# A fused scan, attention and feed-forward kernel: the two heads' TensorE products issued one behind the other

## The chip, the core and the metric

The kernel runs on one core of one Trainium2 chip. The metric is the device time of one execution in microseconds (us). TensorE is PE in the profile, its weight loads PEld, VectorE is DVE, ScalarE is ACT, GpSimd is POOL, and SyncE (SP) issues most of the DMAs. `s`, `pt`, `av`, `y`, `f` and so on are tiles; a number behind L is a line of the kernel.

## The reference, cut to what matters

The input is x of shape (8, 384, 32, 32) in float32: eight images of 1024 tokens with 384 channels. Layer 0 is a bidirectional state-space scan with 16 states per channel, a depthwise convolution and a gate. Layer 1 is causal attention with six heads of 64 channels, then a feed-forward part with quantized activations (the feed-forward part is zero for the last three images). The attention, which the change touches:

```python
scores = jnp.einsum('bhqd,bhkd->bhqk', q, k)
causal = jnp.tril(jnp.ones((T, T), dtype=bool))
scores = jnp.where(causal, scores, -jnp.inf)
attn = jax.nn.softmax(scores, axis=-1)
out = jnp.einsum('bhqk,bhkd->bhqd', attn, v)
```

## The kernel before

Channels lie on the partitions, 128 at a time, so an image has three blocks `c` of channels and a block holds two heads, `e` = 0 on partitions 0 to 63 and `e` = 1 on 64 to 127. The tokens are cut in halves `g` or `h` of 512 and in tiles of 128.

The scan is cut into 768 units of two states each. For a unit POOL multiplies (L587, `g`), ACT makes two exponentials (L600, `da`), DVE scans twice (L605), POOL multiplies again (L611), and PE transposes `g` into the PSUM bank `y` with eight products (L619). The tile `g` has six buffers; a buffer is free again when PE has transposed it. When the last state of a channel block is summed, `s_gate` (L640) builds `yb` in a PSUM bank with PE and DVE reads it (L667).

Attention of one image goes through the three blocks `c` and the two halves `g`. `scores` (L768) handles 128 queries and up to 512 keys for both heads: a score product per head (L779, contracting 64 partitions), on the diagonal a mask added by a further product (L788), then per head the negated row maximum on DVE (L798) and the exponential with its row sum on ACT (L799). The score tiles `ss` of the two heads take both banks of the tag `s`. `weighted_values` (L809) turns the probabilities with PE transposes into the two banks of the tag `pt` (L851), copies them on ACT (L853, `ptn`), and `weigh` (L856) multiplies them with the values (L863): both heads write one bank `av`, each its own half of the partitions. `spread` (L830) lays the row factors out in a bank `f` (L836), which ACT copies (L843).

PSUM has eight banks: one for `y`, two for `da`, two for `s`, two for `pt`, one for `av` (L95). The helper `bank` (L98) takes a tag; without a tag it takes `s` and `pt` in turn, so that `f` and `yb` fall on either. The feed-forward part takes `s`, and the preparation of later images' scans takes `pt` and `av`.

What sets the order: the program is written as lists of steps with assumed times (in us), and the lists are merged by those times (`spread_over` L1069, `timed` L1145), so that scan units, attention, feed-forward and the preparation of later images are woven together. The framework's scheduler then fixes each engine's order when the program is built, by the order in which instructions were written, by what is ready in its own model, and by two handles: `tc.high_priority(offset=n)` treats instructions as if they had been written n instructions earlier, and `pin` (`tc.keep_in_program_order`) lets an instruction follow the one written just before it on the same engine; other instructions may still come between. An engine then takes its instructions strictly in the fixed order. The last image's attention (L1157) runs without a scan beside it.

Of the kernel before, what the change touches and what calls it, by code (L numbers as in the profile page):

```python
# [2 lines left out]

# [37 lines left out]
PARTS = ((0, 0), (0, 1), (1, 1), (1, 0))  # L41
JOINT = 0.6
SET = 8
AHEAD = 2
ORDER = (0, 1, 2, 3, 5, 6, 4, 7)
LOG_EXP = "natural_log_exp_and_others"
# [7 lines left out]
def kernel(  # L54
# [43 lines left out]
    def bank(name, tag=None):  # L98
        if tag is None:
            turn[0] += 1  # L100
            tag = ("s", "pt")[turn[0] % 2]
        return ps.tile([P, HB], F32, name=name, tag=tag, bufs=BANKS[tag])
# [4 lines left out]
    def chunk(c):  # L107
        return slice(c * P, (c + 1) * P)
# [531 lines left out]
    def s_gate(u):  # L640

        if not u.last:
            return
        b, c, h = u.b, u.c, u.h
        yts = sst.pop(("yt", b, c, h))
        both = []
        for what in ("us", "z"):
            t = sp.tile([P, HB], F32, name=f"{what}h_{u.name}", tag=what, bufs=1)
            load(t, spilled[b, what, c][:, half(h)])
            both.append(t)  # L650
        us, sz = both
        tp = bank(f"yb_{u.name}")
        nc.tensor.matmul(
            out=tp, lhsT=diagd[:, c, :], rhs=us, start=True, stop=False, skip_group_check=True
        )
        for yt in yts:
            for i in range(QT):
                nc.tensor.matmul(
                    out=tp[:, chunk(i)],
                    lhsT=yt[:, i, :],  # L660
                    rhs=ident,
                    is_transpose=True,
                    start=False,
                    stop=(yt is yts[-1] and i == QT - 1),
                    skip_group_check=True,
                )
        nc.vector.tensor_tensor(sz, sz, tp, ALU.mult)  # L667
        t = dram.tile([P, HB], F32, name=f"sgy_{u.name}", tag=f"sp_gy_{c}_{h}")
        nc.sync.dma_start(out=t, in_=sz)
        spilled[b, "gy", c, h] = t  # L670


    def attention(b, emit_ffn, emit):
# [80 lines left out]

        def rows_of(e):
            return slice(e * HD, (e + 1) * HD)

# [3 lines left out]
        def probabilities(c, g, steps):  # L763


            nb = g + 1

            def scores(i, qi, n, kb, k0, k1):  # L768
                pr = mtile(f"pr_{b}_{c}_{qi}_{kb}").rearrange("p (e l) -> p e l", e=2)
                st["pr", c, g, i, kb] = pr  # L770
                if kb == 0 and i == 0:
                    for what in ("nm", "rs"):
                        st[what, c, g] = small.tile(
                            [P, QT, 2, nb], F32, name=f"{what}_{b}_{c}_{g}", tag=f"{what}{nb}"
                        )
                nm, rs = st["nm", c, g], st["rs", c, g]
                ss = [bank(f"s_{b}_{c}_{qi}_{kb}_{e}", "s") for e in range(2)]
                for e in range(2):
                    nc.tensor.matmul(  # L779
                        out=ss[e][:, : k1 - k0],  # L780
                        lhsT=st["q"][rows_of(e), c, chunk(qi)],
                        rhs=st["k"][rows_of(e), c, k0:k1],
                        start=True,
                        stop=(k1 < n),
                    )
                if k1 == n:
                    for e in range(2):
                        nc.tensor.matmul(  # L788
                            out=ss[e][:, k1 - k0 - P : k1 - k0],
                            lhsT=identb,  # L790
                            rhs=cmaskb,
                            start=False,
                            stop=True,
                        )
                for e in range(2):
                    s = ss[e][:, : k1 - k0]
                    m = nm[:, i, e, kb : kb + 1]
                    nc.vector.tensor_reduce(m, s, AX.X, ALU.max, negate=True)  # L798
                    nc.scalar.activation(  # L799
                        pr[:, e, : k1 - k0], s, AF.Exp, bias=m, accum_out=rs[:, i, e, kb : kb + 1]  # L800
                    )

            for i in range(QT):
                qi = g * QT + i
                n = (qi + 1) * P
                for kb, (k0, k1) in enumerate(blocks_of(n)):
                    steps(lambda i=i, qi=qi, n=n, kb=kb, k0=k0, k1=k1: scores(i, qi, n, kb, k0, k1))

        def weighted_values(c, g, steps):  # L809


            last = (g + 1) * QT - 1

            def factors():

                nm, rs = st["nm", c, g], st["rs", c, g]
                st["f", c, g] = mtile(f"f_{b}_{c}_{g}").rearrange("p (k l) -> p k l", k=2)
                if g == 0:
                    nc.vector.reciprocal(rs, rs)
                    return  # L820
                low = small.tile([P, QT, 2, 1], F32, name=f"low_{b}_{c}", tag="low")
                nc.vector.tensor_reduce(low, nm, AX.X, ALU.min)
                nc.vector.tensor_tensor(nm, low.to_broadcast([P, QT, 2, 2]), nm, ALU.subtract)
                nc.scalar.activation(nm, nm, AF.Exp)
                nc.vector.tensor_tensor(rs, rs, nm, ALU.mult)
                nc.vector.tensor_reduce(low, rs, AX.X, ALU.add)
                nc.vector.reciprocal(low, low)
                nc.vector.tensor_tensor(rs, nm, low.to_broadcast([P, QT, 2, 2]), ALU.mult)

            def spread(kb):  # L830

                fp = bank(f"f_{b}_{c}_{g}_{kb}")
                for i in range(QT):
                    for e in range(2):
                        f = st["rs", c, g][:, i, e, kb : kb + 1]
                        nc.tensor.matmul(  # L836
                            out=fp[rows_of(e), chunk(i)],
                            lhsT=f.to_broadcast([P, HD]),
                            rhs=ident,
                            start=True,  # L840
                            stop=True,
                        )
                nc.scalar.copy(st["f", c, g][:, kb, :], fp)  # L843

            def turned(j):
                cols = slice(max(j - g * QT, 0) * P, HB)
                for e in range(2):
                    pt = bank(f"pt_{b}_{c}_{g}_{j}_{e}", "pt")
                    for i in range(max(j - g * QT, 0), QT):
                        pr = st["pr", c, g, i, j // QT]  # L850
                        nc.tensor.transpose(pt[:, chunk(i)], pr[:, e, chunk(j % QT)], ident)  # L851
                    ptn = ptp.tile([P, HB], F32, name=f"ptn_{b}_{c}_{g}_{j}_{e}", tag=f"ptn{e}")
                    nc.scalar.copy(ptn[:, cols], pt[:, cols])  # L853
                    st["ptn", j, e] = ptn

            def weigh(j):  # L856
                if j % QT == 0:
                    st["av"] = bank(f"av_{b}_{c}_{g}_{j}", "av")
                av = st["av"]
                cols = slice(max(j - g * QT, 0) * P, HB)  # L860
                for e in range(2):
                    hd = 2 * c + e
                    nc.tensor.matmul(  # L863
                        out=av[rows_of(e), cols],
                        lhsT=st["v"][:, j, hd * HD : (hd + 1) * HD],
                        rhs=st["ptn", j, e][:, cols],
                        start=(j % QT == 0),
                        stop=(j % QT == QT - 1),
                    )
                if j % QT < QT - 1:  # L870
                    return
                kb = j // QT
                o, f = st["o"][:, c, half(g)], st["f", c, g][:, kb, :]
                if kb == 0:
                    nc.vector.tensor_tensor(o, av, f, ALU.mult)  # L875
                else:
                    nc.vector.tensor_tensor(av, av, f, ALU.mult)
                    nc.vector.tensor_tensor(o, o, av, ALU.add)

            for j in range(last + 1):  # L880

                @steps
                def _(j=j):
                    if j == 0:
                        factors()
                    if j % QT == 2:
                        spread(j // QT)
                    turned(j)
                    if j > 0:
                        weigh(j - 1)  # L890

            @steps
            def _():
                weigh(last)
# [314 lines left out]
```

## Time and profile before

| what | us |
|---|---|
| median of 4 runs (lowest, highest) | 5205.45 (5194.56, 5219.49) |
| the profiled execution, and its span | 5209.51, 5207.7 |
| busy PE, DVE, ACT, POOL in the span | 4286.2, 3568.9, 2717.6, 3688.5 |
| score products L779, mask products L788, `av` products L863 (busy) | 467.4, 75.7, 384.7 |
| transposes `y` L619 (busy) | 937.2 |
| attention's seven stretches together | 1987 |

The stretches are those between an image's first score product and its last `av` product: 925 to 1159, 1630 to 1877, 2330 to 2587, 3047 to 3302, 3755 to 4360 (two images), 4478 to 4699 and 5020 to 5188 us. A row of the timeline gives start, length, engine, line, operation, tile written and tiles read, shapes and the number of instructions that were merged; in brackets stands the idle time of the engine before it and what ended it. One float32 product of one head shows as two instructions. A row of the waits gives who waited, for whom, the total, how often and the longest. The granted clock is the share of full TensorE speed.

### The profile page before, as it was taken

The numbers are of one execution on the slowest core, as the hardware profiler recorded it, in microseconds if no ns is written. First come the engines' busy times: TensorE is split into PE (matmuls) and PEld (weight loads), VectorE is DVE, ScalarE is ACT, GpSimd is POOL, SyncE is SP. The second block draws the span as 40 slices with busy tenths as digits, with TensorE's granted clock in tenths as the row PEclk, the third lists the DMA queues.
The fourth block names the chain that finished last, engine by engine and source line by source line (L and its number), as shares of the span: only waits on it lengthen the run. The fifth ranks groups of instructions, "written<-read, shape, count | busy, mean of one in ns | idle before, by whom it ended". The sixth has DMA issues, their size and how long they took to land.

```text
span 5207.7 us, 51029 instructions
## 1 busy us (share of the span) xinstructions
PE 4286.2 (82%) x16842; PEld 2247.5 (43%) x16842; DVE 3568.9 (69%) x4205; ACT 2717.6 (52%) x4898; POOL 3688.5 (71%) x1944
## 2 busy tenths in 40 slices
PE   3677787888878888888887888978888888888799
PEld 1333344444434444444443444434444444444444
DVE  6887887667886577876677856678766655565522
ACT  4565564555644556545555445465454454463334
POOL 0578677886678776887776787677878977787600
PEclk7788787989888899888898898988999989999899
DMA  6554545324463234543243632335433234224200
GB/s 234 204 180 152 195 170 181 112 82 153 151 215 108 85 111 137 193 146 112 101 145 126 209 128 94 102 131 198 142 119 129 89 106 159 85 74 152 82 35 25
DMA packets 365009, 696.38 MB, mean 134 GB/s; under 512 B 30104, under 2 KB 88904, under 8 KB 364744
## 3 DMA queue, kind: packets, MB, share of 16 engines
q1 hardware_dynamic: 355232, 676.97, 38.4%
q10 hardware_dynamic: 9512, 16.15, 0.9%
q8 instruction: 133, 2.18, 0.2%
q14 instruction: 132, 1.08, 0.1%
HBM read 527.33 MB, written 165.68 MB: 133 GB/s over the span
## 4 chain that ended last, share of the span: by engine, by line
POOL 36%; PE 20%; DVE 17%; issue 17%; ACT 6%; DMA 3%; SPq 0%; POOLq 0%; ACTq 0%; DVEq 0%
POOL g L587 19%; POOL g L611 17%; DVE g L605 6%; PE qp L724 3%; PE y L619 3%; PE av L863 2%; PE s L779 2%; PE yp L1024 2%; DVE loc L399 2%; DVE dp L525 2%; PE pt L851 1%; PE ap L920 1%; DVE du L527 1%; DVE u L368 1%; PE op L694 1%
## 5 line engine op out<-in xcount | busy, mean ns | idle before, releaser
L587 POOL TENSOR_TENSOR g<-ud,bc 128x1024 f32<-128x1024 f32 x768 | 1835.0, 2389 | 753.7 <-PE y L619 604.3
L611 POOL TENSOR_TENSOR g<-g,bc 128x1024 f32<-128x1024 f32 x768 | 1819.2, 2369 | 255.0 <-DVE g L605 205.2
L600 ACT ACTIVATE da<-dl,amat 128x512 f32<-128x512 f32 x1536 | 1058.5, 692 | 1615.4 <-DVE g L605 1584.7
L605 DVE TENSOR_TENSOR_SCAN g<-da,carry,g 128x512 f32<-128x512 f32 x768 | 954.8, 1271 | 488.2 <-POOL g L587 453.8
L605 DVE TENSOR_TENSOR_SCAN g<-da,g 128x512 f32<-128x512 f32 x768 | 905.9, 1209 | 532.9 <-POOL g L587 510.6
L619 PE MATMUL y<-ident,g 128*128 128x128 f32 x6144 | 937.2, 300 | 274.5 <-POOL g L611 206.1
L619 PEld LDWEIGHTS y<-ident,g 128*128 128x128 f32 x6144 | 777.7, 155 | 704.2 <-issue 331.8
L779 PE MATMUL s<-k,q 64*128 64x512 f32 (+3 forms) x1152 | 467.4, 601 | 163.3 <-ACT pr L799 142.4
L798 DVE TENSOR_REDUCE nm<-s 128x1 f32<-128x512 f32 (+3 forms) x576 | 300.5, 545 | 247.7 <-PE s L788 182.3
L799 ACT ACTIVATE pr<-s,nm 128x512 f32<-128x512 f32 (+3 forms) x576 | 328.8, 574 | 146.5 <-DVE nm L798 145.6
L863 PE MATMUL av<-ptn,v 128*64 128x512 f32 (+3 forms) x1152 | 384.7, 565 | 24.2 <-DVE o L875 23.7
L979 PE MATMUL hp<-t,w 128*128 128x512 f32 x720 | 340.1, 616 | 32.4 <-ACT h L987 10.6
L851 PE MATMUL pt<-ident,pr 128*128 128x128 f32 x1728 | 309.7, 301 | 48.5 <-ACT ptn L853 25.3
L1024 PE MATMUL yp<-h,w 128*128 128x512 f32 x720 | 328.8, 614 | 11.2 <-DMA w<-w2s 6.3
L340 PE MATMUL in<-xn,win 128*128 128x512 f32 x576 | 293.9, 654 | 52.7 <-DVE xc L462 16.5
L853 ACT COPY ptn<-pt 128x512 f32<-128x512 f32 (+3 forms) x576 | 261.3, 479 | 122.1 <-PE pt L851 120.6
L779 PEld LDWEIGHTS s<-k,q 64*128 64x128 f32 x1152 | 163.4, 206 | 329.7 <-ACT pr L799 212.1
L724 PE MATMUL qp<-t,wqk 128*128 128x512 f32 x576 | 270.3, 620 | 23.7 <-DVE t L301 18.2
L851 PEld LDWEIGHTS pt<-ident,pr 128*128 128x128 f32 x1728 | 207.1, 151 | 180.3 <-ACT ptn L853 84.5
L399 DVE SCALAR_TENSOR_TENSOR loc<-xn,vec,loc 128x496 f32<-128x496 f32 (+3 forms) x384 | 259.4, 721 | 21.7 <-ACT loc L388 20.4
L610 POOL COPY carry<-g 128x2 f32<-128x2 f32 x384 | 83.5, 218 | 230.3 <-DVE g L605 230.3
L1024 PEld LDWEIGHTS yp<-h,w 128*128 128x128 f32 x720 | 140.2, 199 | 179.4 <-issue 167.4
(158 smaller groups left out, 4844.5 us busy)
## 6 DMA issues: line engine op xcount, KB each, us to landing
bc<-rows SPq DMA_DIRECT2D x512, 512.0 KB, 4.1
dl<-sdl SPq DMA_DIRECT2D x160, 256.0 KB, 2.9
ud<-sud SPq DMA_DIRECT2D x160, 256.0 KB, 2.7
t<-st SPq DMA_DIRECT2D x63, 512.0 KB, 5.3
su<-u SPq DMA_DIRECT2D x48, 512.0 KB, 2.9
du<-su SPq DMA_DIRECT2D x96, 256.0 KB, 4.2
sdl<-du SPq DMA_DIRECT2D x96, 256.0 KB, 3.3
sud<-du SPq DMA_DIRECT2D x96, 256.0 KB, 2.7
```

Of the source, the lines that this page charges most:

```text
L399: nc.vector.scalar_tensor_tensor(to, tap, vec[:, c, V_DW + k : V_DW + k + 1], to, ALU.mult, ALU.add)
L587: pin(nc.gpsimd.tensor_tensor(g, ud, sst["bc", 0, u.b, u.part, u.n], ALU.mult))
L600: nc.scalar.activation(da, sst["dl", u.b, u.c, u.part], AF.Exp, scale=amat[:, u.c, n : n + 1])
L605: nc.vector.tensor_tensor_scan(gi[:, ::step], da[:, ::step], gi[:, ::step], first, ALU.mult, ALU.add)
L611: pin(nc.gpsimd.tensor_tensor(g, g, sst["bc", 1, u.b, u.part, u.n], ALU.mult))
L619: nc.tensor.matmul(out=y[:, j, :], lhsT=g[:, i, chunk(j)], rhs=ident, is_transpose=True, start=(u.opens and i == 0 and j == 0), stop=(u.cl ...
L724: nc.tensor.matmul(out=qp, lhsT=st["wqk"][:, c, o : o + P], rhs=st["xn"][:, c, half(h)], start=(c == 0), stop=(c == NC - 1),)
L779: nc.tensor.matmul(out=ss[e][:, : k1 - k0], lhsT=st["q"][rows_of(e), c, chunk(qi)], rhs=st["k"][rows_of(e), c, k0:k1], start=True, stop=(k ...
L851: nc.tensor.transpose(pt[:, chunk(i)], pr[:, e, chunk(j % QT)], ident)
L863: nc.tensor.matmul(out=av[rows_of(e), cols], lhsT=st["v"][:, j, hd * HD : (hd + 1) * HD], rhs=st["ptn", j, e][:, cols], start=(j % QT == 0 ...
L979: nc.tensor.matmul(out=hp, lhsT=st["w1"][:, c, chunk(m % 2)], rhs=st["xn"][:, c, half(h)], start=(c == 0), stop=(c == NC - 1),)
L1024: nc.tensor.matmul(out=yp, lhsT=st["w2", k // 6][:, k % 6, :], rhs=st["h", k // NC][:, k % NC, half(h)], start=(k == 0), stop=(k == NF - 1),)
```

## The change

The second head's product is given a priority 400 instructions earlier and is pinned behind the first head's, and head 1 comes first, in the score products and in the `av` products. The masks are pinned behind both score products, head 1's first. Head 1's exponential is pinned behind head 0's. `yb` and `f` always take the tag `pt`, so the turn between `s` and `pt` shifts for the tiles that still alternate.

```diff
+HURRY = 400
...
-        tp = bank(f"yb_{u.name}")
+        tp = bank(f"yb_{u.name}", "pt")
...
+        def at_once(second):
+            return tc.high_priority(offset=HURRY) if second else nullcontext()
...
-                for e in range(2):
-                    nc.tensor.matmul(
-                        out=ss[e][:, : k1 - k0],
-                        lhsT=st["q"][rows_of(e), c, chunk(qi)],
-                        rhs=st["k"][rows_of(e), c, k0:k1],
-                        start=True,
-                        stop=(k1 < n),
-                    )
+
+                order = (1, 0)
+                for e in order:
+                    with at_once(e == order[1]):
+                        mm = nc.tensor.matmul(
+                            out=ss[e][:, : k1 - k0],
+                            lhsT=st["q"][rows_of(e), c, chunk(qi)],
+                            rhs=st["k"][rows_of(e), c, k0:k1],
+                            start=True,
+                            stop=(k1 < n),
+                        )
+                    if e == order[1]:
+                        pin(mm)
                 if k1 == n:
-                    for e in range(2):
-                        nc.tensor.matmul(
+                    for e in order:
+                        mm = nc.tensor.matmul(
...
                         )
+                        pin(mm)
                 for e in range(2):
...
-                    nc.scalar.activation(
+                    exp = nc.scalar.activation(
                         pr[:, e, : k1 - k0], s, AF.Exp, bias=m, accum_out=rs[:, i, e, kb : kb + 1]
                     )
+                    if e == 1:
+                        pin(exp)
...
-                fp = bank(f"f_{b}_{c}_{g}_{kb}")
+                fp = bank(f"f_{b}_{c}_{g}_{kb}", "pt")
...
-                for e in range(2):
+                for e in (1, 0):
                     hd = 2 * c + e
-                    nc.tensor.matmul(
...
+                    with at_once(e == 0):
+                        mm = nc.tensor.matmul(
...
+                    if e == 0:
+                        pin(mm)
```

More of the change, by code (lines that the diff above doesn't have):

```diff
@@ L1 @@
 import itertools
-from contextlib import ExitStack
+from contextlib import ExitStack, nullcontext
 import concourse.bass as bass
@@ L860, in weigh @@
                 cols = slice(max(j - g * QT, 0) * P, HB)
-                for e in range(2):
+                for e in (1, 0):
                     hd = 2 * c + e
[L863 to L869, printed above, removed]
+                    with at_once(e == 0):
+                        mm = nc.tensor.matmul(
+                            out=av[rows_of(e), cols],
+                            lhsT=st["v"][:, j, hd * HD : (hd + 1) * HD],
+                            rhs=st["ptn", j, e][:, cols],
+                            start=(j % QT == 0),
+                            stop=(j % QT == QT - 1),
+                        )
+                    if e == 0:
+                        pin(mm)
                 if j % QT < QT - 1:
```

## The prediction

> **What bounds the kernel now.** I read the page's chain of work first, then the waits of POOL and of PE, then busy time by stage, and last the timeline of PE, where the two heads' products can be seen.
>
> The chain that ended last, by line, on the page:
>
> ```profile
> POOL 36%; PE 20%; DVE 17%; issue 17%; ACT 6%; DMA 3%; SPq 0%; POOLq 0%; ACTq 0%; DVEq 0%
> POOL g L587 19%; POOL g L611 17%; DVE g L605 6%; PE qp L724 3%; PE y L619 3%; PE av L863 2%; PE s L779 2%; PE yp L1024 2%; DVE loc L399 2%; DVE dp L525 2%; PE pt L851 1%; PE ap L920 1%; DVE du L527 1%; DVE u L368 1%; PE op L694 1%
> ```
>
> The scan's two POOL products lead. But POOL is not always at work; the waits of POOL, longest first (total, times, longest):
>
> ```profile
> POOL g L587 <- PE y L619: 604.3, 226, 10.2
> ```
>
> So a POOL product waits 604 us for PE's transposes `y`, which free the buffers of `g`. PE issues in order, so whatever stands ahead of those transposes delays POOL. The waits of PE:
>
> ```profile
> PE y L619 <- POOL g L611: 206.1, 85, 14.3
> PE s L779 <- ACT pr L799: 142.4, 119, 6.0
> ```
>
> POOL and PE wait for each other; PE's second largest wait is for a score bank that the exponential has not yet released. I then took the seven stretches in which attention runs (columns: stretch, length, busy PE, PEld, DVE, ACT, POOL, granted clock, DMA share, GB/s); the first, the last and the sum:
>
> ```profile
> 925.00:1159.00 234.00, 194.09 (x1035) 106.91 (x1034) 152.01 (x191) 135.75 (x318) 193.17 (x100) 0.88 0.28 94
> ...
> 5020.00:5188.00 168.00, 158.63 (x707) 69.44 (x706) 48.65 (x104) 82.12 (x230) 0.00 (x0) 0.91 0.03 10
> sum 1987.00, PE 1690.03 PEld 911.88 DVE 1186.20 ACT 1074.95 POOL 1440.12; mean PE 241.43 PEld 130.27 DVE 169.46 ACT 153.56 POOL 205.73
> ```
>
> In the first six PE is busy 1531 of 1819 us (84%) and POOL 1440 (79%); in the last there is no scan, and PE has 94%. PE work taken out of these stretches shortens the last one nearly whole and the others in part; POOL leaves room for it, 379 us.
>
> Now what the change is about. PE's timeline, a tied product of each kind, and one that is not:
>
> ```profile
> 992.46 1.08 PE L863 MATMUL av<-ptn,v 128*64 128x512 f32 x4
> ...
> 1012.04 1.13 PE L779 MATMUL s<-k,q 64*128 64x512 f32 x4
> ```
>
> ```profile
> 1018.51 1.79 PE L779 MATMUL s<-k,q 64*128 64x512 f32 x4 [2.75 <-ACT pr L799]
> ...
> 1025.80 1.07 PE L863 MATMUL av<-ptn,v 128*64 128x512 f32 x2
> ```
>
> One head's product is two instructions, so x4 is a pair and x2 is one head. The pair at 992.46 takes 1.08 us, and so does the single head at 1025.80: two heads side by side on different halves of the array cost what one costs. The pair at 1018.51 has nothing between its heads, yet takes 1.79: its second head waited for its bank.
>
> Counted in the trace (a tied pair's two heads start within 45 ns): of 288 score pairs 88 run side by side, 68 follow each other with the second one late, 132 have other PE work between the heads. Of 288 `av` pairs 179 run side by side and 109 don't.
>
> **Part 1, the `av` products (L863).** The transposed probabilities of head 0 are copied by ACT ahead of head 1's. Today head 0's product may go when its copy is there, and older work slips in before head 1's. The change issues head 1 first, whose input comes last, and head 0 right behind it; then both inputs are there, and I expect all 109 to run side by side. By shape, untied pairs by what one head holds PE (start to start at high clock): 51 of 512 by 1.00, 22 of 384 by 0.80, 28 of 256 by 0.58, 8 of 128 by 0.37: 51.0 + 17.6 + 16.2 + 3.0 = **88 us of PE**. Cost: the first product now waits for the second copy (0.585 us for 512 columns, L853); behind it in PE's queue stand transposes and `y`, but a copy made for step j is used one step later, and PE and its weight loads wait for such a copy at `av` only 2.5 us in all, so I put the wait at 0 and its bound at 109 x 0.585 = 64 us.
>
> **Part 2, the score products (L779, L788).** Untied: 102 of 512 by 1.06, 30 of 384 by 0.84, 30 of 256 by 0.63, 38 of 128 by 0.42, which is 108.1 + 25.2 + 18.9 + 16.0 = 168 us if every one of the 200 ran side by side, 0.84 each. It can't be taken whole. Both need a bank of the tag `s`, which has two, and these come free one after the other, when ACT has done head 0's exponential and then head 1's. What keeps a pair apart is mostly that, and priority does not bring the second bank sooner. What the tie does bring is that the two maxima and the two exponentials then follow each other closely, so that the banks of the next pair come free closely too: today a late second head makes a late exponential and again a late second head. I take the 132 split pairs: half run side by side, 66 x 0.84 = 55; half become like the pair at 1018.51, which costs 1.79 in place of twice 1.06, about 0.38 of the gain, 66 x 0.32 = 21. The 68 that already follow each other stay. Sum **76 us**, bounds 0 and 168.
>
> The second product's priority lets it pass older PE work, `y` among it; that work then waits one product, at most 1.06 us, and no PE work is added: 0. The masks (L788) are tied behind both products. Head 0's maximum then waits for head 1's product as well, up to 1.06 us later than now where the pair was split; DVE is at 65% and has the scan to do meanwhile. I put it at 0.
>
> **Part 3, `f` and `yb` leave the banks of `s` for those of `pt`.** By PE's waits, `s` waits for `yb`'s reader 9.5 us (DVE zh L667) and, at 512 columns, for `f`'s 4.9 (ACT f L843); `pt` waits for `f`'s reader 16.4 and for `yb`'s 5.9. About half of the `f` and `yb` were in `pt` already, so the first sum goes and the second may double: -14.4 + 22.3, so I take **8 us** lost, bounds -25 and +25. Other tiles that take `s` and `pt` in turn change places; nothing in the trace prices that, and it lies within the same bounds.
>
> **Part 4, the exponential of head 1 tied behind head 0's.** They run in that order wherever I looked; 0.
>
> Sum of PE work: 88 + 76 - 8 = 156 us less. The last stretch holds about 15% of it (its untied heads hold PE 85 us of the 555 that all untied heads hold, both lines) and takes it whole: 24. In the others a part turns into waits for exponentials, which come no sooner: I take 0.65 of 132, that is 86, between 0.4 (53) and 1 (132). Together 110. The profiled execution took 5209.5 us around a span of 5207.7: 5209.5 - 110 = 5099.5. The median of the runs shown, 5205.45, is 4 us below the profiled one, hence about **5095 us**.
>
> A denser PE might be granted less clock: the same form took 1.78 us at 1022.60 and 1.07 at 1025.80. The stretches' means run from 0.84 to 0.92; a shift of 0.02 on 1690 us of PE work is 38 us either way, and is in the range.
>
> One rule speaks against the score term. An exponential of 512 columns takes 0.680 us and its accumulator's reading 0.196, so a pair holds ACT 1.75 us, more than the 1.06 of its product. The Trainium skill, TensorEngine Tiling, section PSUM Bottleneck, says that tiling speeds up TensorE but not the emptying of PSUM. By that rule the 76 us would be nothing and the result that of the first rival below; by the rows, ACT is busy 136 of 234 us in the first stretch and so bounds a single pair, not the stage.
>
> **The rivals.**
> *Only `av` is tied in effect.* For: 119 waits of `s` on `pr`, the two banks. Against: the 88 pairs that do run side by side now, with the same banks. 88 us of PE, by the same conversion (13 in the last stretch, 0.65 of 75): 62 off the median, 5143.
> *Nearly all is tied.* If close exponentials keep the banks together, 88 + 168 = 256 us of PE, 38 of them in the last stretch and 0.65 of 218: 180 off, 5025. Against: the 68 pairs that follow each other today and still wait.
> *Slower: the tie locks the banks.* A pair takes both banks and gives both back late, and PE, in order, stands before the pair with `y` behind it and POOL behind `y`. Price: one exponential with its reading, 0.876 us, for half of the 252 pairs beside the scan is 110, less the 62 of `av`: 48 more, about 5253. It decides once the idle time before L779 grows from 142 us by more than the 156 us of work removed. For it: the longest such wait is already 6.0 us.
> *The tie does nothing.* The scheduler may find no free bank and put other work between as before, with the bank moves costing what `av` gains: 5205.
>
> **The numbers.** Forecast 5095 (5050 to 5125), 0.40; only `av`, 0.24; nearly all, 0.15; slower, 0.13; nothing, 0.08. The range reaches from 4995 (most of the third case) to 5215 (the last and all of `av`). A measurement of this kernel tells about 0.3%, 16 us, from no change: faster 0.79, same 0.08, slower 0.13.
>
> **What would show it.** PE's busy time on L863 falls from 384.69 us by about 90, on L779 from 467.43 by about 75; rows of x2 become x4 with about 1.1 us; POOL's wait for `y` falls from 604 by about 80; the last stretch falls from 168 to about 145. If L779's busy time stays and PE's wait for `pr` stays, the first rival holds; if that wait passes 300 us, the slower one. I am wrong in the conversion if PE's busy time falls as said and the span does not.

## The result and the profile after

The changed kernel takes 5217.41 us (median of 49 runs, 5199.11 to 5234.35), the kernel before 5206.28 us (73 runs). The ratio is 1.0021, with a 95% interval of 1.0015 to 1.0027: a loss of 0.2%, which counts as no change by the bound of 0.3% that the prediction set, where it forecast 2.1% less. The profiled execution took 5210.11 us with a span of 5208.3.

The chain of work that ended last, on the page of the changed kernel:

```profile
POOL 39%; PE 18%; DVE 17%; issue 17%; ACT 5%; DMA 3%; SPq 0%; POOLq 0%; ACTq 0%; DVEq 0%
POOL g L588 19%; POOL g L612 19%; DVE g L606 5%; PE qp L725 3%; PE yp L1039 2%; PE y L620 2%; PE pt L863 2%; DVE loc L400 2%; PE s L786 2%; PE av L876 1%; DVE dp L526 1%; PE ap L935 1%; DVE u L369 1%; DVE du L528 1%; PE hp L994 1%
```

The `av` products fell from 2% to 1%, the transposes `pt` rose from 1% to 2%, and POOL's share grew from 36 to 39%. The groups of the two kinds of product (busy us and mean ns, then the idle time before them):

```profile
L786 PE MATMUL s<-k,q 64*128 64x512 f32 (+3 forms) x1152 | 426.5, 638 | 197.2 <-ACT pr L809 187.6 <-DVE v L750 4.9 <-ACT v L750 4.2
...
L876 PE MATMUL av<-ptn,v 128*64 128x512 f32 (+3 forms) x1152 | 273.7, 559 | 32.6 <-ACT ptn L865 31.9 <-DVE o L890 0.6
```

`av` is busy 111 us less than before (384.7), the score products 41 us less (467.4). So the change does what it says. But the waits did not shrink. POOL's for PE, then PE's (total, times, longest):

```profile
POOL g L588 <- PE y L620: 622.1, 176, 18.8
```

```profile
PE s L786 <- ACT pr L809: 187.6, 122, 6.5
PE pt L863 <- ACT ptn L865: 82.0, 60, 5.2
```

POOL waits 622 us for the transposes in place of 604, less often and longer at a time; PE waits 45 us longer for score banks and 57 us longer for the copies of the transposed probabilities. The stretches with attention, the first, the last and the sum of seven (length, busy PE, PEld, DVE, ACT, POOL, granted clock, DMA share, GB/s):

```profile
922.00:1164.00 242.00, 181.45 (x1040) 109.35 (x1039) 157.56 (x195) 138.25 (x322) 198.80 (x103) 0.87 0.26 89
...
5016.00:5192.00 176.00, 148.83 (x708) 70.20 (x708) 47.16 (x104) 80.10 (x229) 0.00 (x0) 0.79 0.03 10
sum 1979.00, PE 1571.64 PEld 915.05 DVE 1209.58 ACT 1066.39 POOL 1442.52; mean PE 224.52 PEld 130.72 DVE 172.80 ACT 152.34 POOL 206.07
```

PE is busy 118 us less in them, and they are 8 us shorter. The last one, with no scan to wait for, became longer (168 to 176 in these windows), with its clock down from 0.91 to 0.79.

**Where the gain went.** Busy time times mean granted clock is taken here as a rough measure of PE's work at full clock. The score tie is what the change does to the score products, masks and exponentials, the `av` tie what it does to the `av` products. The three profiled executions:

| | before | changed | without the score tie (e5) |
|---|---|---|---|
| span | 5207.7 | 5208.3 | 5136.4 |
| PE busy | 4286.2 | 4178.4 | 4206.2 |
| granted clock | 0.883 | 0.870 | 0.880 |
| work (busy x clock) | 3785 | 3635 | 3701 |
| span less busy | 921.5 | 1029.9 | 930.2 |

From before to the changed kernel work fell by 149.5, which at the old clock is 169 us of busy time. 61 us of it came back because the clock was lower (4178.4 less 3635.2/0.883), and 108 us became idle time: -169 + 61 + 108 = 0. In e5, described below, less work is taken out (94 us at the old clock), but only 14 us come back by the clock and 9 us as idle time, and 71 us remain. This is bookkeeping with mean clocks, not yet a cause; added up piece by piece over the clock records, work fell by 149 as well.

### The profile page after: what moved, and what is told of

Its sections match the earlier page's. It is cut to its first block, busy times and chain, and to the rows that moved or that the text cites. A ratio compares the mean times of both kernels' runs of the same rounds, so it can differ in the third digit from the quotient of the medians.

```text
span 5208.3 us, 51090 instructions
## 1 busy us (share of the span) xinstructions
PE 4178.4 (80%) x16842; PEld 2259.5 (43%) x16842; DVE 3595.5 (69%) x4206; ACT 2702.2 (52%) x4891; POOL 3687.3 (71%) x1944
## 3 DMA queue, kind: packets, MB, share of 16 engines
q14 instruction: 132, 1.08, 0.1%
## 4 chain that ended last, share of the span: by engine, by line
POOL 39%; PE 18%; DVE 17%; issue 17%; ACT 5%; DMA 3%; SPq 0%; POOLq 0%; ACTq 0%; DVEq 0%
POOL g L588 19%; POOL g L612 19%; DVE g L606 5%; PE qp L725 3%; PE yp L1039 2%; PE y L620 2%; PE pt L863 2%; DVE loc L400 2%; PE s L786 2%; PE av L876 1%; DVE dp L526 1%; PE ap L935 1%; DVE u L369 1%; DVE du L528 1%; PE hp L994 1%
## 5 line engine op out<-in xcount | busy, mean ns | idle before, releaser
L620 PE MATMUL y<-ident,g 128*128 128x128 f32 x6144 | 954.2, 303 | 299.9 <-POOL g L612 234.3
L620 PEld LDWEIGHTS y<-ident,g 128*128 128x128 f32 x6144 | 801.9, 157 | 645.5 <-POOL g L612 351.2
L786 PE MATMUL s<-k,q 64*128 64x512 f32 (+3 forms) x1152 | 426.5, 638 | 197.2 <-ACT pr L809 187.6
L863 PE MATMUL pt<-ident,pr 128*128 128x128 f32 x1728 | 336.2, 315 | 94.8 <-ACT ptn L865 82.0
L863 PEld LDWEIGHTS pt<-ident,pr 128*128 128x128 f32 x1728 | 217.9, 158 | 269.4 <-ACT ptn L865 169.5
L876 PE MATMUL av<-ptn,v 128*64 128x512 f32 (+3 forms) x1152 | 273.7, 559 | 32.6 <-ACT ptn L865 31.9
L1039 PEld LDWEIGHTS yp<-h,w 128*128 128x128 f32 x720 | 139.0, 197 | 176.0 <-issue 164.8
```

The costliest lines, as they stand in the source:

```text
L620: nc.tensor.matmul(out=y[:, j, :], lhsT=g[:, i, chunk(j)], rhs=ident, is_transpose=True, start=(u.opens and i == 0 and j == 0), stop=(u.cl ...
L786: mm = nc.tensor.matmul(out=ss[e][:, : k1 - k0], lhsT=st["q"][rows_of(e), c, chunk(qi)], rhs=st["k"][rows_of(e), c, k0:k1], start=True, st ...
L1039: nc.tensor.matmul(out=yp, lhsT=st["w2", k // 6][:, k % 6, :], rhs=st["h", k // NC][:, k % NC, half(h)], start=(k == 0), stop=(k == NF - 1),)
```

## The experiments

Ratios are to the kernel before, run on the same chip, with the 95% interval.

### One part at a time: e1, e2, e3, e4

Theory L was that the score tie puts the two banks in step and eats what the `av` tie gains; theory M that the bank moves cost; theory N that PE time is worth nothing here.

e1 is the kernel before with the `av` hunk alone:

```diff
-                for e in range(2):
+                for e in (1, 0):
...
+                    with at_once(e == 0):
...
+                    if e == 0:
+                        pin(mm)
```

> The kernel before with the tie of the two av products alone. All 288 av pairs side by side, busy time of the av line down from 385 us to about 280, as in the changed kernel; score products as before. Theory L (the score tie puts both score banks in step and its waits eat what the av tie gains): faster, 25 to 60 us (ratio 0.988 to 0.995). Theory M (f and yb in the banks of pt are what costs): the same 25 to 60 us faster. Theory N (PE time is worth nothing here, POOL and the exponentials set the pace, and a lower granted clock takes the rest): within 0.3%.

Measured: 5170.65 us, ratio 0.9942 (0.9924 to 0.9959). All 288 pairs run side by side, and the line is busy 277.9 us. PE time seems to be worth something, so theory N falls, if e12 below is kept in mind.

e2 has the score hunk alone (order, priority, pins of the second product, the masks and the exponential):

```diff
+                order = (1, 0)
+                for e in order:
+                    with at_once(e == order[1]):
...
+                    if e == 1:
+                        pin(exp)
```

> The kernel before with the score products, masks and exponentials tied, av and the banks as before. Theory L: slower by 0.4 to 1%, PE's wait for the exponentials before the score products up from 142 us to 180 or more, and the last stretch (168 us before) longer by 5 us or more. Theory M: faster by 0.3 to 1%. Theory N: within 0.3%.

Measured: 5349.06 us, ratio 1.0284 (1.0263 to 1.0304), far beyond the 0.4 to 1% that theory L had expected. POOL's wait for the transposes, and the last stretch:

```profile
POOL g L588 <- PE y L620: 715.9, 177, 21.7
```

```profile
5130.00:5322.00 192.00, 164.83 (x699) 72.21 (x698) 47.03 (x104) 81.11 (x229) 0.00 (x0) 0.81 0.03 9
```

The wait rose by 112 us from 604.3 with fewer waits (177 for 226): they became long ones. The last stretch is longer by 24 us (168 before), more than theory L's 5. But PE's wait for the exponentials rose only from 142 to 161, less than the 180 that theory L had asked for.

e3 has the bank moves alone:

```diff
-        tp = bank(f"yb_{u.name}")
+        tp = bank(f"yb_{u.name}", "pt")
...
-                fp = bank(f"f_{b}_{c}_{g}_{kb}")
+                fp = bank(f"f_{b}_{c}_{g}_{kb}", "pt")
```

> The kernel before with yb and f always in the banks of pt, nothing tied. Theory M: slower by 0.4 to 1%, PE's wait for the copies of the transposes up from 25 us to 60 or more. Theory L and theory N: within 0.3%.

Measured: 5224.78 us, ratio 1.0046 (1.0028 to 1.0064), as theory M had it; but PE's wait for the copies was 34 us, not 60.

e4 is the changed kernel with these two lines undone:

> The changed kernel with yb and f taking s and pt in turn as before. Theory M: faster than before by 0.5 to 1%. Theory L: like the changed kernel, within 0.3% of before or slower. Theory N: within 0.3%.

Measured: 5273.76 us, ratio 1.0141 (1.0122 to 1.0161). Theory M falls: taking the moves out makes the changed kernel slower, not faster. The parts do not add up. Alone the moves cost 0.46%; beside both ties they gain 1.2%. The score tie costs 2.0% beside the `av` tie (1.0141 over 0.9942).

### What the score tie costs beside the other two parts: e5, e6

> The changed kernel without the score tie: av tied, yb and f in the banks of pt. If the parts add up (av alone gave 0.9942, the bank moves alone 1.0046): ratio 0.997 to 1.001, and the score tie of the changed kernel costs some 0.2 to 0.4% beside them. If the bank moves only help together with the score tie: 1.000 to 1.005. If they help the av tie: below 0.994.

e5 is the changed kernel with the score hunk undone, that is, e1 and e3 together. Measured: 5135.37 us, ratio 0.9851 (0.9831 to 0.9872), which is what the last of the three expectations said: the moves help the `av` tie. So within this change the score tie costs 1.7% (1.0021 over 0.9851), and the other two parts alone would have brought 1.5%. Its waits and its last stretch:

```profile
POOL g L588 <- PE y L620: 570.4, 222, 12.3
```

```profile
PE s L783 <- ACT pr L803: 138.8, 121, 6.0
PE pt L855 <- ACT ptn L857: 50.0, 40, 5.0
```

```profile
4967.00:5120.00 153.00, 144.13 (x708) 65.57 (x707) 49.18 (x104) 80.77 (x229) 0.00 (x0) 0.92 0.03 11
```

The last stretch begins 49 us earlier than in the changed kernel (first score product at 4967.8 against 5016.9) and is 23 us shorter (151.9 against 174.8, first score product to last `av`): together the 72 us by which the spans differ. POOL's wait for PE is 52 us shorter, and 5 of its waits for the transposes `y` are longer than 8 us in place of 18 in the changed kernel (49 us in all in place of 233). So two thirds of the cost lie beside the scan.

What PE does while POOL waits can be read in the same traces. In the changed kernel PE stands idle for only 24 of the 622 us, and 2 of these are waits for exponentials; in the 18 long waits it is idle 6 of 233 us, and most of its products there are `pt`, `av`, `f` and `s`. So POOL then waits behind a long row of attention work, not behind a PE that stands before the score banks at that time. PE stands at other times, which may help to bring its transposes late: before the last image its waits for exponentials at `s` are 34 us longer than in e5, and its waits for the copies at `pt` and `av` 57 us longer.

e6 takes the tie of the exponentials out of the changed kernel:

```diff
-                    if e == 1:
-                        pin(exp)
```

> The changed kernel without the tie of the exponentials. In the order of PE that was fixed when the program was built, 211 score pairs stand next to each other instead of 260, and the longest runs of other PE work between two scan transposes are 56, 56, 39, 33 matmuls, where the changed kernel has 62, 62, 59, 46 and the score tie alone 98, 92, 84, 83. Theory Q (the tie makes long runs of attention work in PE's queue, the scan's POOL products, with six buffers, run dry behind them): faster than the changed kernel by 15 to 40 us, ratio 0.994 to 0.999, POOL's longest wait for PE below 15 us (18.8 in the changed kernel). Theory S (the two score banks come free in step, PE idles between pairs): no faster than the changed kernel, the last stretch stays at 170 us or more.

Measured: 5190.06 us, ratio 0.9955 (0.9937 to 0.9972), 0.66% below the changed kernel; POOL's longest wait for PE is 11.3 us. This is what theory Q expected, though 0.66% is not much more than the 0.42% that e12 below gives to chance. The last stretch took 168 us and its clock was 0.82, a little better than theory S had said.

### Four score banks where no scan runs: e7, e9, e10

In the last image the banks of `da` are idle. e7 is the changed kernel with

```diff
-                ss = [bank(f"s_{b}_{c}_{qi}_{kb}_{e}", "s") for e in range(2)]
+                turn_of[0] ^= b == ORDER[-1]
+                tag = ("s", "da")[turn_of[0]]
+                ss = [bank(f"s_{b}_{c}_{qi}_{kb}_{e}", tag) for e in range(2)]
```

> The changed kernel; in the last image, where no scan runs, score pairs take the banks of s and of da in turn, so that four banks serve them. Theory S: the last stretch falls from 175 us to 130 to 145, PE's idle time in it from 27 to below 15 us, its granted clock rises from 0.79 to 0.87 or more; ratio 0.993 to 0.997. If the last stretch is long for another reason (transposes waiting for their copies): it stays above 165.

Measured: 5155.77 us, ratio 0.9892 (0.9873 to 0.9910). The last stretch, and a piece of its PE timeline:

```profile
5024.00:5137.00 113.00, 111.18 (x708) 55.69 (x707) 47.16 (x104) 78.32 (x229) 0.00 (x0) 1.00 0.04 15
```

```profile
5039.48 1.13 PE L789 MATMUL s<-k,q 64*128 64x512 f32 x4
5040.54 0.44 PE L866 MATMUL pt<-ident,pr 128*128 128x128 f32 x2
5040.90 0.92 PE L789 MATMUL s<-k,q 64*128 64x384 f32 x4
```

113 us with a granted clock of 1.00, shorter than any theory had it: the next pair starts 1.42 us after the last one, and does not wait for its exponentials. With two banks, in the changed kernel:

```profile
5026.03 2.63 PE L786 MATMUL s<-k,q 64*128 64x512 f32 x4 [1.28 <-ACT pr L809]
5028.60 0.40 PE L797 MATMUL s<-cmaskb,identb 128*128 128x128 bf16 x2
5028.79 0.64 PE L863 MATMUL pt<-ident,pr 128*128 128x128 f32 x2
5031.08 2.74 PE L786 MATMUL s<-k,q 64*128 64x512 f32 x4 [1.66 <-ACT pr L809]
```

The pairs are tied (x4), each starts only when ACT gives the banks back, PE stands 1.3 to 1.7 us before each, and the pair itself takes 2.6 to 2.7 us in place of 1.1. Two things lengthen it: its second head starts 0.56 and 0.67 us after the first, one exponential later, and the clock is granted at one half here (5021.8 to 5038.9 us). The first is theory S, seen in place.

e9 is e1 with the same four banks:

> The kernel before with av tied and four score banks in the last image, score products not tied. Theory S: last stretch from 154 us (av tied alone) to 135 to 148, ratio 0.990 to 0.993. If only tied pairs suffer from the banks: unchanged, 0.994.

Measured: 5132.66 us, ratio 0.9842 (0.9820 to 0.9863). This is a larger gain than theory S had expected (135 to 148 us, 0.990 to 0.993). The last stretch of e1, then of e9:

```profile
4994.00:5148.00 154.00, 144.48 (x699) 66.42 (x697) 48.72 (x103) 80.86 (x229) 0.00 (x0) 0.87 0.03 11
```

```profile
4999.00:5115.00 116.00, 113.69 (x698) 55.98 (x698) 46.16 (x104) 77.85 (x229) 0.00 (x0) 1.00 0.04 15
```

So untied pairs suffer from two banks as well, and with four, tied pairs (113) are hardly quicker than untied ones.

e10 adds the bank moves, which makes it e5 with four banks:

> av tied, yb and f in the banks of pt, four score banks in the last image, score products not tied. If the gains add up (0.9851 for the first two; four banks took 38 us more where av alone was tied): ratio 0.976 to 0.980, last stretch 110 to 118 us. If the last stretch's gain was already in the 0.9851: 0.983 to 0.986.

Measured: 5124.85 us (five runs, 5100.08 to 5125.50), ratio 0.9826 (0.9805 to 0.9848), the fastest version of all, though not clear of e9. The gains of e5 and of the four banks do not add up (that would have been 0.976 to 0.980). The last stretch fell to 119 us, but began at 4988.4, 21 us later than in e5; why is open. Against e7, which has the score tie besides, it is 0.7% faster, and all of that lies ahead of the last stretch, which begins at 5024.6 in e7.

### The clock by itself: e13

e13 adds work to the changed kernel that nobody needs, in the last image behind each score pair:

```diff
+                if b == ORDER[-1]:
+                    for r in range(1):
+                        idle = bank(f"idle_{c}_{qi}_{kb}_{r}", "da")
+                        pin(nc.tensor.matmul(out=idle, lhsT=ident, rhs=st["q"][:, c, half(0)], start=True, stop=True))
```

> The changed kernel with 36 products added in the last image, one of 128x512 behind each score pair, into a bank of da that nobody reads: 31 us more PE work at full clock. Theory C (the idle time between pairs lowers the granted clock and this lengthens the last stretch): the clock in it rises from 0.79 to 0.87 or more and it grows by less than 12 us, from 175 to at most 187. If the clock has no part in it or stays low: 195 us or more.

Measured: 5217.22 us, ratio 1.0017 (1.0004 to 1.0029). The last stretch, and its timeline:

```profile
5019.00:5184.00 165.00, 155.50 (x778) 72.58 (x778) 47.58 (x104) 80.34 (x229) 0.00 (x0) 1.00 0.03 10
```

```profile
5027.33 1.69 PE L786 MATMUL s<-k,q 64*128 64x512 f32 x4 [0.63 <-ACT pr L813]
5028.95 0.28 PE L797 MATMUL s<-cmaskb,identb 128*128 128x128 bf16 x2
5029.07 1.08 PE L808 MATMUL idle<-q,ident 128*128 128x512 f32 x2
```

With 36 useless products more, the stretch is 10 us shorter than in the changed kernel (164.7 against 174.8, first score product to last `av`). Its clock is 1.00, and the pair with its wait for the second bank takes 1.69 us in place of 2.63. What theory C expected came about: PE work put into the gaps keeps the clock up, and the lower clock had lengthened the pairs. But idle time alone does not set the clock. The stretch with the filler has 9.5 us of it, none longer than 1.0 us, at a clock of 1.00; e1's last stretch has 9.5 us too, none longer than 1.1, at 0.87. What in the filler makes the difference is not shown. Over the whole kernel the 10 us are 0.2%, within what its runs vary; the stretch itself shows them.

### Chance of the order, and POOL's buffers: e11, e12, e14 to e17

e11 sets the priority of the second head to zero:

```diff
-HURRY = 400
+HURRY = 0
```

> The changed kernel with the earlier rank of the second head set from 400 to 0: only the pins remain. PE's fixed order has its longest runs without a scan transpose at 75, 62, 62, 59, 48 matmuls (62, 62, 59, 46, 43 in the changed kernel). Theory Q (these runs are the cost): not faster than the changed kernel, ratio to before 1.000 to 1.010. If the earlier rank itself, passing the transposes, is the cost: faster than the changed kernel by 0.5% or more, ratio below 0.997.

Measured: 5240.59 us, ratio 1.0065 (1.0047 to 1.0083), as theory Q had it; passing the transposes by 400 is not what costs. POOL's longest wait for PE rose to 27.8 us.

e12 shifts a turn and changes nothing else:

```diff
-    turn = [0]
+    turn = [1]
```

> The kernel before with the turn of the untagged tiles started at 1 in place of 0, so that each of them takes the other of s and pt; the same work and no tie. A measure of what a mere reshuffle of the fixed order does. If effects of about 0.5%, as the bank moves alone showed, are chance of the order: it lies up to 0.5% off 1. If the order is steady against such changes: within 0.2%.

Measured: 5228.71 us, ratio 1.0042 (1.0029 to 1.0056), and POOL's wait for the transposes is 639.9 us in place of 604.3. This is a warning for every line above. One reshuffle of the fixed order moves this kernel by 0.4%, and another may move it by more, so the 0.46% of e3 need not be a price of the moves, and e1's gain of 0.58% is hardly clear of it. The effects of 1% and more stand clear of it. To test the largest one, e14 and e15 shift the same turn in the changed kernel and in e5:

> The changed kernel with the turn of the untagged tiles started at 1. That start alone moved the kernel before by 0.42%. If the score tie's cost (1.7% between the changed kernel and the one without it) is real: this one stays 1% or more above its partner without the score tie. If a good part was chance of the order: within 0.8% of it.

> The partner: av tied, yb and f in the banks of pt, no score tie, the turn started at 1. If 0.9851 is robust: 0.981 to 0.990. If it was partly a lucky order: 0.990 to 0.997, like av tied alone.

Measured: 1.0016 (1.0003 to 1.0028) and 0.9884 (0.9865 to 0.9902), 5216.46 and 5146.83 us: 70 us, 1.3%, between them. The score tie's cost is real, and so is the gain of the other two parts. The long waits repeat as well: 18 of over 8 us in e14 and 5 in e15 (10 in e12).

e16 and e17 are the same two kernels (turn unshifted) with one buffer less for `g`:

```diff
-        g = sp.tile([P, 2, HB], F32, name=f"g_{u.name}", tag="g", bufs=6)
+        g = sp.tile([P, 2, HB], F32, name=f"g_{u.name}", tag="g", bufs=5)
```

> The changed kernel with five in place of six buffers for g, which lets POOL run ahead of PE by one unit less. Theory Q (long runs without a scan transpose starve POOL): the gap to its partner without the score tie grows from 82 us to 100 or more. Theory S (the score banks in step, whatever POOL does): the gap stays at 60 to 95.

> The partner: av tied, yb and f in the banks of pt, no score tie, five buffers for g. Both theories: slower than with six buffers by 1 to 5%; theory Q: less slowed than the changed kernel is.

Measured: 5235.54 us (1.0057, 1.0041 to 1.0074) and 5144.13 us (0.9870, 0.9849 to 0.9891). The gap is 91 us, 1.9% where it is 1.7% with six buffers. It lies within the 60 to 95 us that theory S had expected and short of the 100 of theory Q, which so failed its own test; as 9 us are less than what a reshuffle moves, the pair does not decide. In the profiles the part of the gap before the last stretch grew from 49 to 78 us (first score product of the last image at 5055.4 and 4977.9), which leans to Q, but with the 20 us or so by which e12 differs it proves nothing. e17 also fell short of the 1% of slowing that both theories had expected: five buffers cost 0.2%.

## Why the prediction was wrong, point by point

**Part 1, the `av` products: right in effect.** All 288 pairs run side by side; 88 us of PE were expected, the line is busy 111 us less (part of that is the overlap of the rows' modelled ends). The wait put at 0 is 31.9 us in the changed kernel, within its bound of 64 (4.9 us in e1, without the score tie).

**Part 2, the score products: right about the order, wrong about the pairs.** Other work stands between the heads in 28 pairs in place of 132. But some 20 more run side by side, where 66 were taken, and 41 us of busy time went in place of 76. The prediction's 88 tied pairs count late ones in part, those whose second head starts with the second half of the first. By the first instruction of each head 76 pairs ran side by side and 80 had a late second head; in the changed kernel it is 95 and 165. "Both come free closely" was no argument: the second bank still comes one exponential after the first, and the tie cannot change that. (The 0.38 of the gain for a late pair goes by the start of the next product, 1.72 us after the pair's; by the 1.79 that is quoted it would be 0.31.)

**Part 3, the bank moves: not measurable alone.** 8 us were taken as lost; e3 shows 0.46%, e12 shows that 0.42% can come from the order. Beside the `av` tie the moves gain 0.9% (e5 over e1), which the prediction did not have.

**Part 4, the exponentials tied: put at 0, and probably wrong.** Without this tie the changed kernel is 0.66% faster (e6), against the 0.42% of e12.

**The sum of PE's work: right in size.** 156 us were expected to go; 169 us went, at the old clock.

**The conversion: this is the step that failed.** "I take 0.65 of 132, that is 86, between 0.4 (53) and 1 (132)" and, for the last stretch, "takes it whole: 24". It was 0 all told: the part ahead of the last stretch became 6 us shorter (its first score product at 5016.9 for 5022.8) and the last stretch 10 us longer (174.8 for 164.8). Even the `av` tie alone gained only 30 us (0.58%, e1) where its 88 us would have given 62 by this conversion. In the last stretch, which was to fall by about 24 us, the runs show how: the tie makes the pair wait for both banks, PE stands idle before each pair (27 us in place of 9, first score product to last `av`), and the clock was granted at 0.79 in place of 0.91. The shift of the clock was in the prediction as an error either way with an unknown sign; in this stretch it went down, and e13 shows that useless work in the gaps brings it back. Beside the scan the shape of the loss is shown (PE waits longer for exponentials and copies, and POOL's waits for `y` become fewer and longer, 5 over 8 us in e5 and 18 in the changed kernel, with PE at work in them), and that the score tie brings it (e5, and e14 with e15). How it does so is not settled. Theory Q, that the fixed order now has long runs of attention work without a transpose, fits these long waits; it also fits e6 and e11, whose orders were counted before they ran, and e2, which had already run. But e16 and e17 came out within theory S's range, and no run shortens the runs and keeps the tie.

**The rivals.** "The tie does nothing" (5205) came nearest in number, by luck: the ties took effect, and what they gained went again. "The tie locks the banks" was right in part. It had 48 us more; the measured change is 11 more. Its mechanism is what the last stretch shows. Beside the scan it had PE standing before the pair with POOL behind it, and the traces show PE at work while POOL waits. It was to decide once PE's wait for score banks grew by 156 us; that grew by 45, but the copies of the transposes added 57, the `av` copies 31 and the clock 61. Its price per exponential, 0.876 us, is too high: in the traces the next exponential of 512 columns starts 0.68 us after the last (5030.25 and 5030.93 in the changed kernel), since the reading of the sum overlaps it. The rule on emptying PSUM that was weighed against the score term pointed the right way: in the last stretch, with four banks to empty in place of two (e7), the tied kernel lost 63 us of its 175, and its clock was full.

**What the prediction named as its sign of being wrong came out:** PE's busy time fell, on the `av` line by 111 us for 90 and on the score line by 41 for 75, and the span did not, which was to mean a wrong conversion. POOL's wait for `y`, which was to fall by 80 us, rose by 18, and the last stretch, which was to fall to 145, took 175.

## What to carry to other kernels

Work taken off a busy engine is worth its time only if the next thing that the engine waits for comes sooner too; before tying two products, count the buffers that they both need, and give the pair a second set where there is room (here this was tried in the last stretch alone, and gained there with and without the tie). Where TensorE has short idle times, look at the granted clock beside the busy time, since a lower clock can return part of what was saved. And where a scheduler fixes the order, measure a change that only reshuffles it: here one such change was worth 0.4%, and no effect of that size could be read from a single version.

## What the runs showed of the hardware

Two products on different halves of the array cost what one costs, in both forms. With 64 partitions contracted into two banks, a pair of heads at 512 columns takes 1.13 us at full clock (e7, at 5039.48) and a single head 1.12 in the kernel before:

```profile
5102.33 1.12 PE L779 MATMUL s<-k,q 64*128 64x512 f32 x2
```

With 64 columns each into one bank it is 1.08 for the pair and 1.07 for the single head (the prediction's rows).

In the last stretch of the changed kernel the clock was granted at one half in pieces of 17 to 24 us, though no idle time of PE in it was longer than 1.7 us; with the filler of e13 the longest was 1.0 us and the clock stayed full. The Trainium skill, TensorE: Matmul & The Clock Gate, section Why this matters for your kernels, asks for no idle gaps over about 3 us between bursts of matmuls. Here the clock was halved in stretches that keep to that, with gaps of up to 1.7 us in the changed kernel and up to 1.1 us in e1; the measurement decides.
